# A convolutional attention kernel: column sums and divisors on quarters of TensorE's columns, inverses spread by DMA

## Chip, cores and metric

One core of a Trainium2 chip runs the whole kernel. The metric is the device time of one execution in microseconds (us). Three runs of the kernel before took 2658.37, 2661.5 and 2662.64 us; the median is 2661.5.

## What is computed

Two layers work on x of shape (8, 512, 64, 64) in float32: 8 images of 512 channels and 4096 positions. The first is softmax attention over max-pooled keys and values, the second is linear attention with a feature map `delu`.

```python
def layer0(x):
    f = conv1x1(x, Wf, bf).reshape(b, c // 8, h * w)
    g = maxpool2x2(conv1x1(x, Wg, bg)).reshape(b, c // 8, hwp)
    v = maxpool2x2(conv1x1(x, Wh, bh)).reshape(b, c // 2, hwp)
    beta = softmax(einsum('bcn,bcm->bnm', f, g), axis=-1)
    o = einsum('bcm,bnm->bcn', v, beta).reshape(b, c // 2, h, w)
    return gamma * conv1x1(o, Wv, bv) + x

def layer1(x):
    Q, K, V = wq x + bq, wk x + bk, wv x + bv
    Qf, Kf = delu(Q).transpose(0, 2, 1), delu(K)
    KV = einsum('bmn,bcn->bmc', Kf, V)
    norm = 1.0 / einsum('bnd,bd->bn', Qf, sum(Kf, axis=-1) + EPS)
    return x + gamma[0] * einsum('bnd,bdc,bn->bcn', Qf, KV, norm)
```

Two kinds of inverses matter here: those of the softmax's sums over the 1024 keys (one for each position), and `norm`, those of the second layer's divisors (one for each position as well).

## The kernel before, in words

An image's 4096 positions are cut into 8 chunks of 512, so there are 64 chunks, `s` = 0 to 63, and `j` = `s` mod 8 is the chunk's place in its image. `step(s)` (the loop over steps is at the end of `run`) lists pieces of work with a due time `t` by `at(t, fn, ...)`, sorts them by `t` and emits them in this order. The order on each engine's queue is thus written out by hand. The due times only order the work; they start nothing.

One step mixes four stages for different chunks:

- Stage A, for a chunk 9 ahead: f and g (`a_fg`, L259) and the values (`a_h`, products H, L303), with the pooled values turned by a DMA transpose (`turn_v`, L358, SP's queue, t = 18.7) and joined by ScalarE (L363).
- For chunk n = s + 1: the weights E = exp of the scores (`weigh`, matmuls `s`, L394), their sum over the keys (`sum_of_e` on VectorE adds the 8 tiles into one, `total` sums over the partitions), the inverses (`invert`), a check value for each chunk (`look`) and the multiplication of E with the inverses in four blocks (`normalize_block`, L460). E has keys on partitions and positions along the free axis, so the inverse of a position has to be on every partition. `total` does this by a matmul with a 128x128 tile of ones: every row of its result is the sum.
- For chunk s: the attention (`attend`, products M1 to M7 of a 2x2 scheme with 7 products, L484, their sums on VectorE), the projection and the residual (`project`, products N, L547). ScalarE evicts N1 three times (L557), GpSimd adds that to `xb` (L560), VectorE adds the others (L563, L568). N6, N5 and N3 accumulate into N1's bank and wait for the evictions.
- Layer 1 for chunk s: features (`features`, matmuls pk, L593, which read the finished `xb`), and for chunk s - 1 the sum of K times x (`gather`, matmuls pg, L687, on two halves of TensorE's columns). For the image before (`b_c`): `normalize` makes the divisors of a pair of chunks (matmul pd, L770), inverts them (L774) and multiplies `qq` with them (L777). It runs at j = 0 for the image's first pair and at j = 1, 3, 5 for the next pair. `finish` at odd j multiplies with KV (matmuls pa, L795), ScalarE copies to `y` (L798), and GpSimd's queue stores 1 MB twice with an accumulating DMA (L801, t = 12.6 and 14.3).

SP's queue issues the other DMAs in order: an output store (L574), loads of the next chunks (L212, L224), four transposes of x and one of k (L648, L630), one of v (L358). A wait of one of them holds all behind it.

Tiles come from pools: `bank` gives one of 8 PSUM banks, `scratch` one of 7 buffers of 128x512, `work1` one buffer for each tag. In the last image (s = 56 to 63) stage A is over and the steps are shorter; the features move into the next step.

After `run`, VectorE tests all of the check values against a limit (`good`, `least`, `bad`), and a second, general version of the whole program is branched over when they are in order, as they are here.

Of the kernel before, what the change touches and what calls it, by code (L numbers as in the profile page):

```python
# [36 lines left out]
F32 = mybir.dt.float32  # L37
U16 = mybir.dt.uint16
AF = mybir.ActivationFunctionType
ALU = mybir.AluOpType  # L40
AX = mybir.AxisListType

PARAM = 10.0
EPS = 1e-10
P = 128
CH = 512
SAFE = 1e27

# [2 lines left out]
def tile_two_attention_blocks(  # L51
# [72 lines left out]
    ident = const.tile([P, P], F32, name="ident")  # L124
# [38 lines left out]
    chk = const.tile([P, 2, TOTAL], F32, name="chk")  # L163

    def half(e):
        return slice(e * D, (e + 1) * D)

    def run(ctx, general):
# [6 lines left out]
        work1 = ctx.enter_context(tc.tile_pool(name="work1", bufs=1))  # L175
        work = ctx.enter_context(tc.tile_pool(name="work", bufs=2))
        temp = ctx.enter_context(tc.tile_pool(name="temp", bufs=7))
        turned = ctx.enter_context(tc.tile_pool(name="turned", bufs=1))
        small = ctx.enter_context(tc.tile_pool(name="small", bufs=4))
        psum = ctx.enter_context(tc.tile_pool(name="psum", bufs=8, space=bass.MemoryType.PSUM))  # L180

        def bank(name):
            return psum.tile([P, CH], F32, tag="m", name=name)

        def scratch(name):
            return temp.tile([P, CH], F32, tag="t", name=name)

# [38 lines left out]
        st = {}  # L226
        fgs, fs, vps = {}, {}, {}

        th, hs, es, sums, totals, rtots, te, os_, to, ns = ({} for _ in range(10))
        pxs, x_last, stored, late = [], {}, {}, {}  # L230
        kTs, xTs, pks, qq, halves, turned_halves = ({} for _ in range(6))

# [204 lines left out]
                nc.vector.tensor_tensor(r[:, 0, :], r[:, 0, :], r[:, 1, :], ALU.add)  # L437

        def total(s):
            pt = totals[s] = bank(f"tot_{s}")  # L440
            nc.tensor.matmul(pt, ones, sums[s][:, 0, :], start=True, stop=True)  # L441

        def invert(s):

            rtots[s] = bank(f"rtot_{s}")
            nc.vector.reciprocal(rtots[s], totals[s])  # L446

        def look(s):
            pt = totals[s]
            nc.scalar.activation(pt, pt, AF.Copy, accum_out=chk[:, 0, s : s + 1])  # L450
            nc.scalar.activation(pt, rtots[s], AF.Copy, accum_out=chk[:, 1, s : s + 1])

        def block(s, i, j):

# [309 lines left out]
        def normalize(pair, at, t, t_invert, t_out):  # L764

            m = {}

            def product():
                m["pd"] = bank(f"pd_{pair}")
                nc.tensor.matmul(m["pd"], kb, qq[pair], start=True, stop=True)  # L770

            def inversion():
                m["rn"] = scratch(f"rn_{pair}")
                nc.vector.reciprocal(m["rn"], m["pd"])  # L774

# [117 lines left out]
        def step(s):  # L893
# [5 lines left out]
            pair = (b_c * NCHUNK + j) // 2  # L899
            work = []  # L900

            def at(t, fn, *args):
                work.append((t, len(work), fn, args))
# [50 lines left out]
                    turn_G(b_c, at, 19.5)  # L954
                    make_KV(b_c, at, 21.4, 30.0)
            if c_here and here and j == 0:
                normalize(pair, at, 5.6, 6.9, 13.2)
            if c_here and here and j % 2 == 1 and j < NCHUNK - 1:
                normalize(pair + 1, at, 3.5, 4.9, 4.95)
            if c_here and here and j % 2 == 1:  # L960
                finish(pair, (0, 1), at, 9.2)
                finish(pair, (2, 3), at, 10.9)
# [20 lines left out]
            if after:  # L983
                n = s + 1
                if here:
                    at(5.7, weigh_two, n, 0)
                    at(7.5, weigh_two, n, 2)
                    for m, t in ((2, 9.3), (4, 10.6), (6, 11.8), (8, 13.1)):
                        at(t, sum_of_e, n, m)

                if not here:
                    t, t_invert = 21.2, 21.25
                elif s == 0:
                    t, t_invert = 21.2, 22.6
                else:
                    t, t_invert = 16.1 if j % 2 == 1 and c_here else 17.85, 18.0
                at(t, total, n)
                at(t_invert, invert, n)
                if not general:
                    at(max(21.5, t_invert + 0.1), look, n)  # L1000
                at(24.3, normalize_block, n, 0, 1)
                at(26.0, normalize_block, n, 0, 0)
                at(27.3, normalize_block, n, 1, 1)
                at(29.2, normalize_block, n, 1, 0)
                at(33.6, sums_of_e, n, 1)
                at(36.0, sums_of_e, n, 2)
# [65 lines left out]
        for s in range(-LEAD, TOTAL + 1):  # L1072
            step(s)
# [5 lines left out]
    with ExitStack() as stack, tc.manual_schedule(engines=ENGINES):  # L1079
        run(stack, general=False)  # L1080

    least = const.tile([1, 1], F32, name="least")
    good = const.tile([1, 2 * TOTAL], F32, name="good")
    nc.vector.tensor_scalar(good, chk[0:1].rearrange("p c s -> p (c s)"), SAFE, None, ALU.is_lt)
    nc.vector.tensor_reduce(least, good, AX.X, ALU.min)
    bad = const.tile([1, 1], mybir.dt.int32, name="bad")
    nc.vector.tensor_scalar(bad, least, 0.5, None, ALU.is_lt)
# [41 lines left out]
```

## Time and profile before

The profiled execution took 2656.62 us, its instructions span 2654.5 us; the difference lies before the first and after the last instruction.

| | before |
|---|---|
| median of three runs | 2661.5 us |
| profiled execution / its span | 2656.62 / 2654.5 us |
| TensorE matmul busy | 2606.4 us (98%) |
| VectorE busy | 2136.8 us (80%) |
| ScalarE busy | 1593.2 us (60%) |
| GpSimd busy | 763.5 us (29%) |
| mean granted TensorE clock | 0.994 |
| reciprocal of the sums (L446), 64 times | 3365 ns each |
| reciprocal of the divisors (L774), 28 times | 3351 ns each |
| `look`'s two passes (L450, L451) | 589 and 582 ns each |
| DMA, mean over the span | 139 GB/s |

How to read it: a float32 matmul appears as two passes, so 64 matmuls are 128 records. Passes overlap at their ends, so the pace of TensorE is read from one start to the next: a pass of 512 columns takes 0.43 us, one of 256 columns 0.216. In the lines of a timeline the columns are the start, the duration (both us), engine, line, operation, output<-inputs, shape and the number of merged instructions; in brackets stands the idle time before and what ended it. In lists of waits the numbers are us in total, times, and the longest. PE is TensorE, DVE VectorE, ACT ScalarE, POOL GpSimd and SP SyncE.

### The profile page before, as it was taken

The page shows a single profiled execution, that of the slowest core. Times are in us where ns is not written, and L with a number is a line of the kernel's source. Part 1 is how long each engine was busy: PE and PEld are TensorE (multiplying, and loading weights), DVE is VectorE, ACT ScalarE, POOL GpSimd, SP SyncE. Part 2 cuts the span into 40 slices and gives each one's busy share as a digit, 9 for nine tenths or more (in the row PEclk, how much of TensorE's full clock was granted, in tenths as well). Part 3 has the DMA queues.
Part 4 walks back from the last instruction along what each step waited for, and adds up shares of the span by engine and source line. Part 5 has one row for each costly group of instructions (what it writes and reads, how often), then busy time and mean ns, then how long its engine had stood idle before and what let it go on. Part 6 is the DMA issues. An engine that isn't in the chain of part 4 may idle for free.

```text
span 2654.5 us, 30415 instructions
## 1 busy us (share of the span) xinstructions
PE 2606.4 (98%) x10650; PEld 1798.1 (68%) x10650; DVE 2136.8 (80%) x2990; ACT 1593.2 (60%) x2670; POOL 763.5 (29%) x610
## 2 busy tenths in 40 slices
PE   8899999999999999999999999999999999999996
PEld 6577666667667667667667676666676676666663
DVE  5788879878888878887888888888788788798873
ACT  3365566566566566575675665666665656756661
POOL 4422323322322323223333223323223232221112
PEclk9999999999999999999999999999999999999998
DMA  5143455465555565655664654756555656455657
GB/s 172 49 134 89 115 135 149 104 164 134 133 157 118 142 167 118 164 133 116 152 162 121 155 125 123 180 116 151 141 118 158 155 119 159 117 138 138 154 144 256
DMA packets 465363, 369.91 MB, mean 139 GB/s; under 512 B 339888, under 2 KB 340400, under 8 KB 465200
## 3 DMA queue, kind: packets, MB, share of 16 engines
q1 hardware_dynamic: 444816, 307.16, 42.6%
q0 software_dynamic: 15232, 58.72, 12.0%
q10 hardware_dynamic: 5152, 1.97, 0.3%
q8 instruction: 87, 1.43, 0.2%
q14 instruction: 76, 0.62, 0.1%
HBM read 151.92 MB, written 134.22 MB: 108 GB/s over the span
## 4 chain that ended last, share of the span: by engine, by line
PE 87%; DVE 6%; DMA 1%; issue 1%; ACT 1%; POOL 0%; SPq 0%; DVEq 0%; POOLq 0%; ACTq 0%
PE M L484 27%; PE N L547 14%; PE H L303 11%; PE s L394 8%; PE pk L593 7%; PE fg L259 7%; PE pg L687 4%; PE pa L795 3%; PE tot L441 2%; PE pkv L752 1%; PE pd L770 1%; DMA xb<-in_x_dram 1%; DVE T L469 1%; DVE T L466 1%; DVE r L434 0%
## 5 line engine op out<-in xcount | busy, mean ns | idle before, releaser
L560 POOL TENSOR_TENSOR xb<-xb,n 128x512 f32<-128x512 f32 x192 | 246.7, 1285 | 553.3 <-ACT n L557 504.2
L484 PEld LDWEIGHTS M<-T,S 128*128 128x128 f32 x1536 | 286.5, 190 | 114.3 <-issue 29.2
L557 ACT ACTIVATE n<-N,gb_v 128x256 f32<-128x256 f32 x384 | 161.2, 471 | 334.1 <-PE N L547 333.2
L484 PE MATMUL M<-T,S 128*128 128x256 f32 x1536 | 358.7, 383 | 0.0
L655 ACT COPY xT<-u 128x1024 uint16<-128x1024 uint16 x252 | 328.2, 1353 | 1.4
L460 DVE TENSOR_TENSOR E<-E,rtot 128x1024 f32<-128x1024 f32 x256 | 305.2, 1214 | 3.8 <-issue 1.6
L642 ACT COPY w<-xb 128x1024 uint16<-128x1024 uint16 x252 | 244.8, 1042 | 81.8 <-DVE xb L563 81.8
L398 ACT ACTIVATE E<-s 128x512 f32<-128x512 f32 x512 | 256.1, 615 | 48.3 <-PE s L394 40.6
L446 DVE RECIPROCAL rtot<-tot 128x512 f32<-128x512 f32 x64 | 215.3, 3365 | 49.4 <-PE tot L441 49.4
L547 PE MATMUL N<-to,w_v 128*128 128x256 f32 x1024 | 243.6, 381 | 3.2 <-ACT n L557 3.0
L563 DVE TENSOR_TENSOR xb<-xb,N 128x512 f32<-128x512 f32 x256 | 175.0, 684 | 84.2 <-POOL xb L560 81.9
L394 PE MATMUL s<-f,g 64*128 64x512 f32 x1024 | 238.1, 602 | 1.9 <-DVE o L493 1.9
L593 PE MATMUL pk<-xb,w_kqk 128*128 128x512 f32 x512 | 231.8, 595 | 8.0 <-DVE xb L568 8.0
L634 POOL COPY kT<-uk 128x512 uint16<-128x512 uint16 x56 | 53.1, 949 | 620.6 <-DMA uk<-wk 620.6
L484 PE MATMUL M<-E,vT 128*128 128x256 f32 x1024 | 231.5, 379 | 0.0
L450 ACT ACTIVATE tot<-tot 128x512 f32<-128x512 f32 x64 | 37.7, 589 | 320.0 <-DVE rtot L446 319.9
L547 PEld LDWEIGHTS N<-to,w_v 128*128 128x128 f32 x1024 | 194.3, 191 | 30.8 <-ACT n L557 4.4
L484 PEld LDWEIGHTS M<-E,vT 128*128 128x128 f32 x1024 | 194.6, 190 | 29.4 <-issue 1.9
L259 PE MATMUL fg<-xa,w_fg 128*128 128x512 f32 x472 | 213.9, 596 | 0.0
L547 PE MATMUL N<-o,w_v 128*128 128x256 f32 x768 | 187.7, 380 | 1.9 <-ACT n L557 1.9
L547 PEld LDWEIGHTS N<-o,w_v 128*128 128x128 f32 x768 | 145.1, 190 | 54.8 <-issue 24.2
L394 PEld LDWEIGHTS s<-f,g 64*128 64x128 f32 x1024 | 94.7, 186 | 116.5 <-issue 90.6
(149 smaller groups left out, 4647.8 us busy)
## 6 DMA issues: line engine op xcount, KB each, us to landing
xb<-in_x_dram SPq DMA_DIRECT2D x64, 1024.0 KB, 5.7
out_dram<-xb SPq DMA_DIRECT2D x64, 1024.0 KB, 5.3
xa<-in_x_dram SPq DMA_DIRECT2D x59, 1024.0 KB, 7.4
out_dram<-y POOLq DMA_DIRECT2D x56, 1024.0 KB, 11.4
w_v<-in_L_conv_wv_dram SPq DMA_DIRECT2D x8, 1024.0 KB, 8.1
x_early<-in_x_dram SPq DMA_DIRECT2D x4, 1024.0 KB, 5.7
u<-w SPq DMA_TRANSPOSE x252, 3.3
x<-out_dram SPq DMA_DIRECT2D x12, 256.0 KB, 10.7
```

The source lines that it names most:

```text
L259: nc.tensor.matmul(fg, w_fg[:, k, :], x_a[a][:, k, :], start=(k == 0), stop=(k == KT - 1))
L303: nc.tensor.matmul(m[i], w_h7[i][:, k, :], th[a][i][:, k, :], start=(k == 0), stop=(k == hk - 1))
L394: nc.tensor.matmul(sc[e], g[half(e), i, :], fs[s][half(e), :], start=True, stop=True)
L398: nc.scalar.activation(es[s][:, 2 * i + e, :], sc[e], AF.Exp)
L446: nc.vector.reciprocal(rtots[s], totals[s])
L460: nc.vector.tensor_tensor(b, b, r, ALU.mult)
L484: nc.tensor.matmul(m[i], v7[i][:, k, :], te[s][i][:, k, :], start=(k == 0), stop=(k == hm - 1))
L547: nc.tensor.matmul(a[:, k, :], w_v7[i][:, bass.ts(k, P)], b, start=not more and k == 0, stop=True, skip_group_check=more or k > 0,)
L560: nc.gpsimd.tensor_tensor(of_x(*ij), of_x(*ij), u, ALU.add)
L593: nc.tensor.matmul(pk, w_kqk[:, i, e * D : (e + 2) * D], x_b[s][:, i, :], start=(i == 0), stop=(i == KT - 1),)
L642: nc.scalar.copy(w, x_b[s][:, k, :].bitcast(U16).rearrange("p (n h) -> p h n", h=2))
L655: nc.scalar.copy(v[:, k], u)
```

## The change

Three parts:

1. The sums (`total`) and the divisors (`product` in `normalize`) are no longer made on 128 rows for 512 positions. TensorE's columns are used in quarters of 32: quarter `i` takes 32 columns of weights and the positions 128 i to 128 i + 127, and writes rows 32 i to 32 i + 31. The result is a 128x128 tile. For the divisors the 32 columns are the middle ones of `kb`, 16 of each of the two chunks.
2. The reciprocals run on the 128x128 tile and write SBUF (`rq`, one buffer for both uses). SP's queue then writes the few rows that differ to DRAM (4 rows of 512 bytes for the sums, 8 for the divisors) and reads them back to all partitions (one DMA for the sums, two for the divisors). ScalarE copies the sums' inverses into a PSUM bank (`keep_inverses`). `look` reads the smaller tiles.
3. The due times of the divisors' three pieces change, for j = 0 from 5.6, 6.9 and 13.2, for odd j from 3.5, 4.9 and 4.95, both to 12.65, 13.7 and 30.9. The test at the end covers all 128 rows, with one transpose on TensorE more.

```diff
         def total(s):
-            pt = totals[s] = bank(f"tot_{s}")
-            nc.tensor.matmul(pt, ones, sums[s][:, 0, :], start=True, stop=True)
+
+            pt = totals[s] = bank(f"tot_{s}")[:, 0:P]
+            for i in range(NT):
+                nc.tensor.matmul(
+                    pt[bass.ts(i, QP), :], ones[:, 0:QP], sums[s][:, 0, bass.ts(i, P)],
+                    start=True, stop=True,
+                )
 
         def invert(s):
-
-            rtots[s] = bank(f"rtot_{s}")
-            nc.vector.reciprocal(rtots[s], totals[s])
+            rq[s] = work1.tile([P, P], F32, tag="rq", name=f"rq_{s}")
+            nc.vector.reciprocal(rq[s], totals[s])
+
+        def spread_inverses(s):
+
+            d = rows.tile([NT, P], F32, tag="rd", name=f"rd_{s}")
+            nc.sync.dma_start(out=d, in_=rq[s][0:P:QP, :])
+            u = rtots[s] = scratch(f"rb_{s}")
+            nc.sync.dma_start(out=u, in_=d.rearrange("(o i) n -> o (i n)", o=1).to_broadcast([P, CH]))
+
+        def keep_inverses(s):
+            u, rtots[s] = rtots[s], bank(f"rtot_{s}")
+            nc.scalar.copy(rtots[s], u)
 
         def look(s):
             pt = totals[s]
             nc.scalar.activation(pt, pt, AF.Copy, accum_out=chk[:, 0, s : s + 1])
-            nc.scalar.activation(pt, rtots[s], AF.Copy, accum_out=chk[:, 1, s : s + 1])
+            nc.scalar.activation(pt, rq[s], AF.Copy, accum_out=chk[:, 1, s : s + 1])
...
             def product():
-                m["pd"] = bank(f"pd_{pair}")
-                nc.tensor.matmul(m["pd"], kb, qq[pair], start=True, stop=True)
+
+                pd = m["pd"] = bank(f"pd_{pair}")[:, 0:P]
+                for i in range(NT):
+                    nc.tensor.matmul(
+                        pd[bass.ts(i, QP), :], kb[:, D - QP // 2 : D + QP // 2],
+                        qq[pair][:, bass.ts(i, P)], start=True, stop=True,
+                    )
 
             def inversion():
-                m["rn"] = scratch(f"rn_{pair}")
-                nc.vector.reciprocal(m["rn"], m["pd"])
+                rd = work1.tile([P, P], F32, tag="rq", name=f"rq_pd_{pair}")
+                nc.vector.reciprocal(rd, m["pd"])
+                d = rows.tile([2 * NT, P], F32, tag="rn", name=f"rn_{pair}_row")
+                nc.sync.dma_start(out=d, in_=rd[0 : P : QP // 2, :])
+                rn = m["rn"] = scratch(f"rn_{pair}")
+                for e in range(2):
+                    row = d.rearrange("(i e) n -> e i n", e=2)[e : e + 1]
+                    nc.sync.dma_start(
+                        out=rn[half(e)].rearrange("p (i n) -> p i n", n=P),
+                        in_=row.to_broadcast([D, NT, P]),
+                    )
...
             if c_here and here and j == 0:
-                normalize(pair, at, 5.6, 6.9, 13.2)
+                normalize(pair, at, 12.65, 13.7, 30.9)
             if c_here and here and j % 2 == 1 and j < NCHUNK - 1:
-                normalize(pair + 1, at, 3.5, 4.9, 4.95)
+                normalize(pair + 1, at, 12.65, 13.7, 30.9)
...
                 at(t, total, n)
                 at(t_invert, invert, n)
+                at(t_invert + 0.01, spread_inverses, n)
+                at(max(23.0, t_invert + 0.02), keep_inverses, n)
...
-    least = const.tile([1, 1], F32, name="least")
-    good = const.tile([1, 2 * TOTAL], F32, name="good")
-    nc.vector.tensor_scalar(good, chk[0:1].rearrange("p c s -> p (c s)"), SAFE, None, ALU.is_lt)
+    least = const.tile([P, 1], F32, name="least")
+    good = const.tile([P, 2 * TOTAL], F32, name="good")
+    nc.vector.tensor_scalar(good, chk.rearrange("p c s -> p (c s)"), SAFE, None, ALU.is_lt)
     nc.vector.tensor_reduce(least, good, AX.X, ALU.min)
+    with tc.tile_pool(name="row", bufs=1, space=bass.MemoryType.PSUM) as last:
+        row = last.tile([1, P], F32, name="row")
+        nc.tensor.transpose(row, least, ident)
+        nc.vector.tensor_reduce(least[0:1], row, AX.X, ALU.min)
```

The number `QP` is 32, `NT` is 4, `D` is 64, `P` is 128 and `CH` is 512. `rows` is a pool of DRAM tiles with two buffers for each tag.

More of the change, by code (lines that the diff above doesn't have):

```diff
@@ L45 @@
 P = 128
+QP = 32
 CH = 512
@@ L179, in run @@
         small = ctx.enter_context(tc.tile_pool(name="small", bufs=4))
+        rows = ctx.enter_context(tc.tile_pool(name="rows", bufs=2, space=bass.MemoryType.DRAM))
         psum = ctx.enter_context(tc.tile_pool(name="psum", bufs=8, space=bass.MemoryType.PSUM))
@@ L227, in run @@
         fgs, fs, vps = {}, {}, {}
-        th, hs, es, sums, totals, rtots, te, os_, to, ns = ({} for _ in range(10))
+        th, hs, es, sums, totals, rq, rtots, te, os_, to = ({} for _ in range(10))
         pxs, x_last, stored, late = [], {}, {}, {}
@@ L1080, in tile_two_attention_blocks @@
         run(stack, general=False)
-    least = const.tile([1, 1], F32, name="least")
-    good = const.tile([1, 2 * TOTAL], F32, name="good")
-    nc.vector.tensor_scalar(good, chk[0:1].rearrange("p c s -> p (c s)"), SAFE, None, ALU.is_lt)
+    least = const.tile([P, 1], F32, name="least")
+    good = const.tile([P, 2 * TOTAL], F32, name="good")
+    nc.vector.tensor_scalar(good, chk.rearrange("p c s -> p (c s)"), SAFE, None, ALU.is_lt)
     nc.vector.tensor_reduce(least, good, AX.X, ALU.min)
+    with tc.tile_pool(name="row", bufs=1, space=bass.MemoryType.PSUM) as last:
+        row = last.tile([1, P], F32, name="row")
+        nc.tensor.transpose(row, least, ident)
+        nc.vector.tensor_reduce(least[0:1], row, AX.X, ALU.min)
     bad = const.tile([1, 1], mybir.dt.int32, name="bad")
-    nc.vector.tensor_scalar(bad, least, 0.5, None, ALU.is_lt)
+    nc.vector.tensor_scalar(bad, least[0:1], 0.5, None, ALU.is_lt)
     again = nc.values_load(bad, min_val=0, max_val=1, skip_runtime_bounds_check_because="0 or 1")
```

## The prediction

> **What bounds the kernel now.** I read the page first: busy shares, then the chain that ended last.
>
> ```profile
> PE 2606.4 (98%) x10650; PEld 1798.1 (68%) x10650; DVE 2136.8 (80%) x2990; ACT 1593.2 (60%) x2670; POOL 763.5 (29%) x610
> ...
> PE 87%; DVE 6%; DMA 1%; issue 1%; ACT 1%; POOL 0%; SPq 0%; DVEq 0%; POOLq 0%; ACTq 0%
> ```
>
> TensorE (PE) is 98% busy and carries 87% of the chain. Next I asked for its waits, and for its instructions in one step in which divisors are made and outputs finished (j = 1, about 1424 to 1466 us).
>
> ```profile
> PE pk L593 <- DVE xb L568: 8.0, 2, 6.6
> ...
> 1433.46 3.60 PE L795 MATMUL pa<-qq,kv 64*128 64x512 f32 x16
> 1436.99 1.94 PE L687 MATMUL pg<-xT,kT 128*64 128x512 f32 x8
> 1438.86 1.99 PE L484 MATMUL M<-T,S 128*128 128x256 f32 x8
> 1440.69 1.02 PE L441 MATMUL tot<-r,ones 128*128 128x512 f32 x2
> 1441.55 3.62 PE L484 MATMUL M<-T,S 128*128 128x256 f32 x16
> ```
>
> The longest item in PE's list of waits is 8.0 us in the whole run, so PE is fed everywhere and time taken off it is time taken off the kernel, while nothing else comes late. What can come late is seen on VectorE (DVE) in the same step:
>
> ```profile
> 1441.82 3.37 DVE L446 RECIPROCAL rtot<-tot 128x512 f32<-128x512 f32 x1 [0.51 <-PE tot L441]
> ...
> 1448.84 1.21 DVE L460 TENSOR_TENSOR E<-E,rtot 128x1024 f32<-128x1024 f32 x1
> ...
> 1459.23 0.87 DVE L568 SCALAR_TENSOR_TENSOR xb<-N,gb_v,xb 128x256 f32<-128x256 f32 x2
> ```
>
> The line at L568 ends at 1460.10 and the features' matmuls, which read its xb, start at 1460.52: 0.4 us of slack. Last, the DMAs of that step:
>
> ```profile
> q1 hardware_dynamic: 5665, 4.15, 34.6%
> q0 software_dynamic: 544, 2.10, 27.2%
> ...
> out_dram<-y POOLq DMA_DIRECT2D x2, 1024.0 KB, 10.3
> ...
> uv<-wv SPq DMA_TRANSPOSE x1, 11.4
> ```
>
> In a step that finishes no outputs the same transpose lands sooner:
>
> ```profile
> uv<-wv SPq DMA_TRANSPOSE x1, 3.4
> ```
>
> The two accumulating stores of 1 MB (q0) make the difference. Packet by packet, q0 runs from 1439.1 to 1450.6 us with packets of 4 KB at 0.33 us each on all 16 engines. The transpose's 512 packets start only when the first store is complete and then go one for one with q0's (48 and 48 in a microsecond).
>
> **What the Trainium skill says.** (1) "TensorEngine Tiling (Array Packing)", Key Properties: tiles run in parallel, but a change of tiling mode drains the engine. The trace agrees with both. pg's 8 passes of 512 columns on two half-width tiles take 1.87 us (1436.99 to 1438.86), where eight in a row, as in tot (0.86 us for two), would take 3.44. The two changes of mode around pg cost 0.34: pa takes 3.53 where 8 x 0.43 = 3.44; pg 1.87 where 1.72; the M after it 1.83 where the M of 16 passes shows 3.45/2 = 1.73. (2) "TensorE: Matmul & The Clock Gate", Measured speedup vs the span model: three column tiles gave 2.38 times. No run here shows more than two. (3) "DMA: Bandwidth & Descriptors", Queues, rings and completion order: an engine takes the queue rows in turn and each ring in order. The one-for-one packets agree. (4) The clock gate page, Part 1: a window of idleness halves the clock. Here pauses of 2.95 us (to 92.3) and 3.38 us (to 133.2) were followed by a granted clock of 0.50.
>
> **The change, part by part.** Coordinates are those of the step shown.
>
> PE, sums. Before, 0.86 us (1440.69 to 1441.55). After, four tiles at once, two passes of 128 columns: half of the 0.216 us that a pass of 256 takes, twice, is 0.22; plus a way in and out, 0.34: 0.56. Gain 0.30 x 64 = 19. If the tiles ran one by one it were 0.86 + 0.34 = 1.20, a loss of 0.34.
> PE, divisors. Before, 0.85 us, alone among full-width work. Now they stand right behind pg, so only one more change of mode is paid: 0.22 + 0.15 = 0.37. Gain 0.48 x 28 (j = 0, 1, 3, 5 of seven images) = 13. Together 33 us off the bound engine.
>
> DVE, reciprocals. 3365 ns for 512 columns; a quarter of that, 0.85 to 0.9, for 128 (pure scaling at the low end). That frees 2.5 us in 64 + 28 places, 230 us in all, but DVE isn't the bound, and what it waits for next is the rows.
>
> ACT. Each look's two passes shrink from 0.59 towards a quarter; the new copy of rtot into a bank costs 0.59. ACT is at 60%: near nothing, except for its place in the order. Queued behind the waiting copy are the evictions of N1, and PE's N6, which accumulates into N1's bank, waits for the first of these.
>
> DMA on a free queue. Step by step: a store's first packet starts 1.0 us after its issue and it lands some 0.5 after the last packet (the 1 MB store at 1305.0: 1306.05, 1310.4). Row out: 1.6 to 2.3. Broadcast back: 128 packets of 2 KB, 8 on an engine at 0.085: 2.2 to 3. In the even steps the reciprocal ends 1.1 us after the sums, the copy takes 0.6, so the first normalization can start about 1.3 us earlier than now. Nothing is late; cost 0. The divisors' DMAs at j = 0 meet the weights' load, which ends about 1396.9 us while that step's normalizations start at 1404.5: also 0.
>
> DMA in the odd steps, where q0 is busy. SP's order is: divisors out, two broadcasts (rn), sums out, broadcast (rb), then the v transpose. Each waits on SP for the one it reads, and all behind it wait too.
> - The divisors' reciprocal ends near 1440.6. Their row lands between 1442.9 (if it only alternates with q0) and 1446 (if it is held as the transpose is).
> - rq is one buffer for both, so the sums' reciprocal waits on DVE until the divisors' row has left (1442.9 to 1446, then 0.9). Behind it stand the sums of M5, M7 and M4, which end at 1448.84 today and at 1450.7 at the latest, before N4 needs them (1451.0): 0.
> - rn: 2 x 64 partitions x 4 runs of 512 bytes = 512 packets, 32 on an engine. One for one with q0, only 9 to 18 of them get through before q0 ends (about 1450.9). The rest need under 1 us: 1451.5. Both bounds meet here, since q0's 32 packets on each engine take their 11 us either way.
> - The sums' row follows in the ring: landed 1452.0. rb is issued at 1452.1, first packet 1453.1, landed 1454.4. Copy to 1455.1.
> - Normalization starts at 1455.15, not 1448.84. From there to the end of L568 lie 11.26 us today, of which 2.05 idle (0.31, 0.56, 1.18), plus the multiplication with rn (0.92, L777), which is moved from an idle place to 30.9: 10.1. L568 ends at 1465.3, not 1460.1; less 0.4 slack, 4.8 us of stall. Inside it lies the pause at N6: due at 1452.75, possible at 1456.0 behind copy and eviction. At 3.2 us it is as long as the pauses that halved the clock; I add 0.2. So 5.0 x 21 (j = 1, 3, 5) = 105.
> At j = 7 there are no divisors. The row goes out near 1.4 us after the sums and rb has 8 packets on an engine at 0.41: rows land 0 to 1 us too late, 0.4 x 7 = 3.
>
> The rest. rn holds a scratch buffer of seven until 30.9, but the seventh buffer after it is asked for only at 35; the bank of rtot is taken later than now: 0. The wider test at the end, a transpose and two short reductions: under 1 us; taken as 1.
>
> Sum: -33 + 105 + 3 + 1 = +76 on the profiled execution's 2656.6 us (span 2654.5), so 2732. That execution lies 5 us under the median of 2661.5, so in terms of the median 2737.
>
> **Rivals.** Likeliest (0.70): the rows are late in the odd steps, 2737. With 3.3 to 7 us of stall in 21 steps (69 to 147) it spans 2699 to 2780.
> Faster (0.15): the rows are in time, because small copies pass the accumulating stores, or rn's packets don't hold up the sums' row. Then 33 - 1 are gained: 2629. It decides at 1449.7: if rb has landed by then in such a step, the normalization starts by 1450.3, and 1448.84 + 0.4 + 2.05 - 0.92 is the latest that costs nothing. For it: a free queue needs only some 5 us. Against it: uv's 11.4 us.
> The tiles don't do what they say (0.10): four columns in turn, each with its mode changes. PE loses 0.34 x 64 + 0.16 x 28 = 26 instead of gaining 33: 2737 + 59 = 2796. Against it: pg's halves do overlap.
> Rows late in every step (0.05): if each DMA took over 4 us, as small ones at the start do (b_h, 4.2), the even steps would lose 1 to 2 us as well: 2770 to 2830.
>
> **How the numbers follow.** Predicted is the likeliest, 2737. The range leaves out the faster case and the far tails, and reaches to the others: 2678 to 2825. About 0.2% (5 us) is what a measurement of this kernel can tell from no change. Faster 0.15, the one case; same 0.02, a balance of gain and a stall of 1.5 us; slower 0.83.
>
> **What would show it.** Right: tot takes about 0.2 us of matmul starts and its neighbours 0.3 more; RECIPROCAL near 0.9 us; rb's landing 2 to 3 us in even steps; in odd steps rn's landing near 8 us or more; ACT's copy waits for rb, PE's N6 for ACT's n, pk for L568, some 5 us a step, in odd steps alone. Wrong: odd steps no longer than now, rb landed within 9 us of the sums everywhere, PE waits as few as before. Then q0 doesn't hold the rows up, and the time is near 2629.

## The result, and the profile after

| | before | after |
|---|---|---|
| median | 2660.45 us (four runs, 2658.37 to 2662.64) | 2791.77 us (four runs, 2788.79 to 2793.62) |
| after / before | | 1.0492, 95% interval 1.0474 to 1.0511 |
| profiled execution / its span | 2656.62 / 2654.5 us | 2791.18 / 2789.0 us |
| mean granted TensorE clock | 0.994 | 0.974 |

The kernel is 4.9% slower. The forecast of 2737 us has the right sign and the right place, but the loss is 131 us where 76 were forecast. The 2791.77 us lie within the forecast's range (2678 to 2825) and above 2780, where its likeliest case ends. The range reached further for rivals that did not come true, so it is luck that the result falls into this part. The page of the kernel after, with its busy times and the chain that ended last by engine and by line:

```profile
PE 2633.6 (94%) x11203; PEld 1801.2 (65%) x11203; DVE 1923.9 (69%) x2991; ACT 1589.8 (57%) x2734; POOL 760.2 (27%) x610
...
PE 65%; DMA 15%; DVE 8%; issue 4%; ACT 3%; POOL 1%; SPq 0%; DVEq 0%; POOLq 0%; ACTq 0%
PE M L501 18%; PE H L305 11%; PE N L564 11%; PE s L396 7%; PE pk L610 7%; DMA rn_row<-rq_pd 5%; DMA rb<-rd 4%; DMA rd<-rq 4%; PE pg L704 4%; PE fg L261 3%; PE pa L826 3%; DVE r L436 1%; DVE E L477 1%; ACT n L574 1%; ACT E L400 1%
```

PE carries 65% of the chain where it carried 87%, and the new rows carry 13%: `rn_row` (the divisors to DRAM), `rd` (the sums to DRAM) and `rb` (the sums back). Who waits for them is in the list of waits of the kernel after (us in total, times, longest):

```profile
ACT rtot L463 <- DMA rb<-rd: 348.2, 64, 10.7
...
DVE E L477 <- ACT rtot L463: 191.1, 63, 7.1
...
DVE rq L452 <- DMA rn_row<-rq_pd: 124.9, 27, 6.2
...
PE N L564 <- ACT n L574: 108.2, 43, 6.5
...
PE pk L610 <- DVE xb L585: 8.2, 2, 6.8
```

Read from the bottom: the features (pk) wait as little as before (8.0 us in two times then, 8.2 now), so that isn't where TensorE stops. It stops at N, 43 times, for ScalarE's eviction `n`, which stands behind ScalarE's copy `rtot`, which waits for the row.

Where the time went shows best by steps, from the first M1 to the next (change against before, both from the profiled executions; "short" steps are those where stage A is over):

| steps | number | forecast, each | measured, each | forecast, sum | measured, sum |
|---|---|---|---|---|---|
| j = 1, 3, 5, images 1 to 6 | 18 | +4.22 | +5.08 | +76.0 | +91.4 |
| j = 1, 3, 5, last image (short) | 3 | +4.22 | +8.24 | +12.7 | +24.7 |
| j = 7, five of them | 5 | +0.1 | +2.44 | +0.5 | +12.2 |
| j = 7 of image 6 (short) | 1 | +0.1 | +8.52 | +0.1 | +8.5 |
| j = 2, 4, 6, images 1 to 6 | 18 | -0.30 | -0.28 | -5.4 | -5.0 |
| j = 0, images 1 to 6 | 6 | -0.78 | -0.40 | -4.7 | -2.4 |
| the rest (start, image 0, the last image's even steps, tail) | | | | -3.1 | +5.1 |
| sum | | | | +76 | +134.5 |

The forecast's column is its own terms: -0.30 and -0.48 for TensorE's two gains, +5.0 for a stall, +0.4 at j = 7. The rest holds a start that is 5.25 us longer before the first M1; in the runs below it changes from -1 to +7 us with no relation to the edits, and its cause isn't settled.

One step of the kind shown for before (step 25, j = 1, which starts at 1136.99 us). TensorE after:

```profile
1149.33 1.94 PE L704 MATMUL pg<-xT,kT 128*64 128x512 f32 x8
1151.20 0.43 PE L789 MATMUL pd<-qq,kb 128*32 128x128 f32 x8
1151.56 1.99 PE L501 MATMUL M<-T,S 128*128 128x256 f32 x8
1153.48 0.43 PE L445 MATMUL tot<-r,ones 128*32 128x128 f32 x8
1153.84 3.72 PE L501 MATMUL M<-T,S 128*128 128x256 f32 x16
...
1164.28 1.03 PE L564 MATMUL N<-to,w_v 128*128 128x256 f32 x4
1168.90 2.56 PE L564 MATMUL N<-to,w_v 128*128 128x256 f32 x8 [3.59 <-ACT n L574]
```

The tiles on four quarters do overlap: eight passes of tot take 0.36 us (1153.48 to 1153.84), where eight passes of 128 columns one after the other would take 0.86 us, by the pace of 0.216 us for 256. Then comes the pause of 3.59 us in N. Its cause runs back through VectorE, ScalarE and SP. VectorE after:

```profile
1151.92 0.95 DVE L796 RECIPROCAL rq_pd<-pd 128x128 f32<-128x128 f32 x1
...
1159.74 0.96 DVE L452 RECIPROCAL rq<-tot 128x128 f32<-128x128 f32 x1 [5.73 <-DMA rn_row<-rq_pd]
...
1168.11 1.22 DVE L477 TENSOR_TENSOR E<-E,rtot 128x1024 f32<-128x1024 f32 x1 [4.09 <-ACT rtot L463]
```

ScalarE after:

```profile
1167.49 0.59 ACT L463 COPY rtot<-rb 128x512 f32<-128x512 f32 x1 [5.95 <-DMA rb<-rd]
1168.01 0.83 ACT L574 ACTIVATE n<-N,gb_v 128x256 f32<-128x256 f32 x2
```

SP's queue after, in this step, in an even step (j = 6, from 1352.39) and in the j = 7 that follows (from 1390.13):

```profile
1152.90 0.62 SPq L798 DMA_DIRECT2D rn_row<-rq_pd  x1
1159.67 1.37 SPq L802 DMA_DIRECT2D rn<-rn_row  x2
1161.14 0.56 SPq L457 DMA_DIRECT2D rd<-rq  x1
1163.97 0.35 SPq L459 DMA_DIRECT2D rb<-rd  x1
...
1368.94 0.56 SPq L457 DMA_DIRECT2D rd<-rq  x1
1370.61 0.34 SPq L459 DMA_DIRECT2D rb<-rd  x1
...
1407.74 0.54 SPq L457 DMA_DIRECT2D rd<-rq  x1
1413.30 0.34 SPq L459 DMA_DIRECT2D rb<-rd  x1
```

The distance from `rd` to `rb` is the time that a row of 2 KB takes to DRAM, since rb's DMA waits for it. It is 1.67 us in the even step and 5.56 at j = 7, where the accumulating stores run. By packets, the first one of the row leaves 1.2 us after its issue in the even step and 4.44 us after it at j = 7. I call this longer wait from the issue to the first packet, here 3.2 us more than on quiet engines, **the hold**. In the j = 1 step the divisors' row takes it (first packet 4.8 us after the issue), and all that stands behind it on SP takes it too.

Last, the clock. Windows of the kernel after, of one width, from the pause on (PE's busy time and matmuls, granted clock, DMA share, GB/s):

```profile
1165.00:1168.41 3.41, 0.31 (x2) 1.00 0.50 112
1168.41:1171.83 3.42, 2.93 (x10) 0.76 0.00 0
1171.83:1175.24 3.41, 3.41 (x14) 0.74 0.00 0
1175.24:1178.65 3.41, 3.41 (x17) 1.00 0.00 0
```

After the pause, a stretch of 3.41 us (1170.2 to 1173.6) ran at half clock. (The granted clock is 0.76 and 0.74 in the two windows that it lies in.) Between the start of image 1 and the last step there are 22 such stretches, 12 of 3.41 us and 10 of 6.83, 109 us in all; before there is none. At half speed 109 us do the work of 55, so up to 55 us are lost to the clock, about a third of what the odd steps and j = 7 lose.

### The profile page after: what moved, and what is told of

It is laid out like the page before. It is cut to its first block, busy times and chain, and to the rows that moved or that the text cites. A ratio compares the mean times of both kernels' runs of the same rounds, so it can differ in the third digit from the quotient of the medians.

```text
span 2789.0 us, 32021 instructions
## 1 busy us (share of the span) xinstructions
PE 2633.6 (94%) x11203; PEld 1801.2 (65%) x11203; DVE 1923.9 (69%) x2991; ACT 1589.8 (57%) x2734; POOL 760.2 (27%) x610
## 4 chain that ended last, share of the span: by engine, by line
PE 65%; DMA 15%; DVE 8%; issue 4%; ACT 3%; POOL 1%; SPq 0%; DVEq 0%; POOLq 0%; ACTq 0%
PE M L501 18%; PE H L305 11%; PE N L564 11%; PE s L396 7%; PE pk L610 7%; DMA rn_row<-rq_pd 5%; DMA rb<-rd 4%; DMA rd<-rq 4%; PE pg L704 4%; PE fg L261 3%; PE pa L826 3%; DVE r L436 1%; DVE E L477 1%; ACT n L574 1%; ACT E L400 1%
## 5 line engine op out<-in xcount | busy, mean ns | idle before, releaser
L564 PE MATMUL N<-to,w_v 128*128 128x256 f32 x1024 | 287.7, 424 | 106.5 <-ACT n L574 106.3
L501 PE MATMUL M<-T,S 128*128 128x256 f32 x1536 | 366.9, 389 | 0.0
L564 PEld LDWEIGHTS N<-to,w_v 128*128 128x128 f32 x1024 | 214.0, 214 | 157.6 <-ACT n L574 124.1
L463 ACT COPY rtot<-rb 128x512 f32<-128x512 f32 x64 | 37.7, 589 | 348.2 <-DMA rb<-rd 348.2
L434 DVE TENSOR_TENSOR r<-E 128x1024 f32<-128x1024 f32 x64 | 78.4, 1225 | 192.4 <-ACT E L400 192.4
L305 PE MATMUL H<-xa,w_h 128*128 128x256 f32 x708 | 180.7, 393 | 0.0
```

What stands on the lines that cost most here:

```text
L305: nc.tensor.matmul(m[i], w_h7[i][:, k, :], th[a][i][:, k, :], start=(k == 0), stop=(k == hk - 1))
L501: nc.tensor.matmul(m[i], v7[i][:, k, :], te[s][i][:, k, :], start=(k == 0), stop=(k == hm - 1))
L564: nc.tensor.matmul(a[:, k, :], w_v7[i][:, bass.ts(k, P)], b, start=not more and k == 0, stop=True, skip_group_check=more or k > 0,)
```

## Experiments

The theory (H): the rows are late because the accumulating stores (q0) are on the DMA engines when they are issued. The rivals: (R1) the queue on SP and the shared `rq` make the sums late, whatever q0 does; (R2) the small DMAs are slow by themselves, or the quarters cost TensorE what they save; (R3) the stores' large packets of 4 KB are what hold the small ones up.

### No stores, or later stores

First the stores were taken out altogether; the second layer's outputs are then not added.

```diff
             def out():
-                nc.gpsimd.dma_start(
-                    out=outr[b, :, ks[0] : ks[0] + 2, bass.ts(jp, 2 * CH)],
-                    in_=m["y"].rearrange("p k e n -> p k (e n)"), accum_op=ALU.add,
-                )
+                pass
```

> The changed kernel without the two accumulating stores of the second layer's outputs (they are left out, so those outputs are not added). Theory H (the rows are held up by the accumulating stores): without them the steps j = 1, 3, 5 fall from 47.0 to about 41.1 us, j = 7 from 43.5 to about 39.7, and the run takes about 2630. Rival Q (the sums' row is late because SP issues it behind the divisors' three DMAs and their waits, stores or not): j = 1, 3, 5 stay at 44 or more and the run at 2720 or more. Rival S (rows through DRAM are too slow by themselves): also no better than 2760.

Measured: 2635.22 us in one run, beside a median of 2659.08 for before on that chip. Steps against before: j = 1, 3, 5 -0.70, even -0.31, short odd -0.04, j = 7 -0.30, short j = 7 +1.28 (its trace has a stretch at half clock there, as in the run with the stores late everywhere, below). The chain by engine and PE's waits at N in this kernel:

```profile
PE 86%; DVE 5%; issue 2%; DMA 1%; ACT 1%; POOL 1%; DVEq 0%; POOLq 0%; ACTq 0%; SPq 0%
```

```profile
PE N L564 <- ACT n L574: 10.0, 8, 4.8
```

With SP's order and the shared `rq` unchanged, DMA's share falls from 15% to 1%, and TensorE's gain of some 0.7 us appears in the odd steps. R1 and R2 are out as the cause by themselves. But 59 MB of transfers are gone from the whole run as well (the tail behind the last step's start is 6.2 us shorter), so next the stores were kept and moved:

```diff
-            at(t + 3.4, out)
+            at(20.6 + 0.05 * ks[0], out)
```

> The changed kernel, whole, with the accumulating stores issued some 10 us later in the step (due at 20.6 and 20.7 instead of 12.6 and 14.3), after the rows have landed. Theory H: all stalls of the odd steps go, 2625 to 2640 us, faster than the kernel before. The moved stores may meet the transposes of x at the end of the step, which would cost up to 2 us in an odd step, 2690 at most. Rivals Q and S: 2760 to 2790 as changed.

Measured: 2668.96 us, ratio 1.0040 (1.0028 to 1.0053): above the expected time. Where stage A runs, the theory held: j = 1, 3, 5 at 41.15 us against 46.97 in the kernel after. But the three short odd steps stayed at +8.38 us each and the short j = 7 at +6.78. A due time orders the work and starts nothing: in those steps GpSimd has no sums of x ahead of the stores, so they left as early as before. So the due times were made to depend on the stage:

```diff
-        def finish(pair, ks, at, t):
+        def finish(pair, ks, at, t, t_out):
...
-            at(t + 3.4, out)
+            at(t_out, out)
...
-                finish(pair, (0, 1), at, 9.2)
-                finish(pair, (2, 3), at, 10.9)
+                finish(pair, (0, 1), at, 9.2, 20.6 if a < TOTAL else 25.8)
+                finish(pair, (2, 3), at, 10.9, 20.7 if a < TOTAL else 25.9)
```

> As the kernel with the stores issued later, but in the last image's odd steps and in the j = 7 step before it, where GpSimd has no sums of x to do and the stores therefore still left early, they are due at 25.8, behind GpSimd's first addition to xb. Theory H: the stalls left over there (3 steps of 8.4 us, and two pauses, 6 us, in j = 7 of the sixth image) go too: 2669 - 30, about 2637, every odd step at or below the kernel before's. If those stalls had another cause (the short steps themselves): 2665.

Measured: 2640.97 us, ratio 0.9938 (0.9925 to 0.9952). The short odd steps are back at before's length (0.00). The short j = 7 stays at +1.73: the trace has a stretch of 3.41 us at half clock there, behind pauses of 0.93 and 1.80 us, where before has pauses of 0.93 and 1.34 us without such a stretch. In exchange the last image's even steps are 2.82 us longer (TensorE pauses there 3.1 us a step, at tot and N, against 0.66 before), and its j = 0 2.39. Its chain by engine:

```profile
PE 82%; DVE 6%; DMA 3%; issue 3%; ACT 2%; POOL 1%; DVEq 0%; ACTq 0%; POOLq 0%; SPq 0%
```

With nothing but two due times changed, the kernel after goes from 4.9% slower to 0.6% faster than before. That settles H: the stores' place in time is the cause.

### Which of the two halves, and in which order

The sums alone (divisors and their due times as before):

```diff
-                pd = m["pd"] = bank(f"pd_{pair}")[:, 0:P]
-                for i in range(NT):
...
+                m["pd"] = bank(f"pd_{pair}")
+                nc.tensor.matmul(m["pd"], kb, qq[pair], start=True, stop=True)
...
-                normalize(pair + 1, at, 12.65, 13.7, 30.9)
+                normalize(pair + 1, at, 3.5, 4.9, 4.95)
```

> Only the sums are changed; the divisors are made, inverted and used as in the kernel before. Theory H: the odd steps j = 1, 3, 5 stall as j = 7 does in the changed kernel, about 3.8 us, because the sums' two DMAs meet the stores without any divisors' DMA ahead: steps of about 45.4 us, 28 x 3.8 - 19 more than before: about 2745. Rival Q: without divisors' DMAs ahead the steps j = 1, 3, 5 are as short as before, 41.6, and the run is at about 2660.

Measured: 2716.34 us in one run. j = 1, 3, 5 are 1.93 us longer than before, a stall of 2.2 with the gain of 0.30 added back. The list of waits of this kernel has PE at N:

```profile
PE N L564 <- ACT n L574: 59.5, 57, 4.2
```

More pauses than after (57 against 43), but about 1.0 us each instead of 2.5. Only two stretches at half clock follow, behind pauses of 4.17 and 3.35 us in short steps; behind those of up to 1.6 us there is none. I expected a longer stall: one hold leaves pauses that mostly don't reach the clock.

The divisors alone (`total`, `invert`, `look` and the test at the end as before, no rows for the sums):

```diff
-            pt = totals[s] = bank(f"tot_{s}")[:, 0:P]
-            for i in range(NT):
...
+            pt = totals[s] = bank(f"tot_{s}")
+            nc.tensor.matmul(pt, ones, sums[s][:, 0, :], start=True, stop=True)
...
-                at(t_invert + 0.01, spread_inverses, n)
-                at(max(23.0, t_invert + 0.02), keep_inverses, n)
```

> Only the divisors are changed (quarters, small reciprocal, rows through DRAM, the moved due times); the sums and their inverses are made as before. Theory H: rn lands late in the odd steps too, but nothing needs it before 30.9, so only the gain on TensorE shows, 0.48 us in 28 steps: about 2647. If the moved multiplication of 0.92 us on VectorE or the late rn costs something, the steps j = 1, 3, 5 are longer than 41.4 and the run takes 2660 to 2700.

Measured: 2639.42 us, ratio 0.9925 (0.9908 to 0.9941). j = 1, 3, 5 are 0.50 us shorter (forecast 0.48) and j = 0 1.09, more than its matmuls: the divisors' matmul no longer waits for `kb`, as it did six times before, for 3.1 us in all. Its page:

```profile
PE 2591.9 (98%) x10818; PEld 1791.6 (68%) x10818; DVE 2062.5 (78%) x2990; ACT 1593.2 (60%) x2670; POOL 763.2 (29%) x610
```

PE loses 14.5 us of busy time against before (2606.4) and stays 98% busy. The divisors' rows have till 30.9 to land and so never stall anyone. The same kernel again, on another chip:

> The kernel with only the divisors changed once more, on the chip of the two others: about 0.9925 of the kernel before, 2638 to 2641.

Measured: 2639.96 us, ratio 0.9934 (0.9919 to 0.9949).

Next, both halves, but the divisors' DMAs behind the sums' on SP and with a buffer of their own:

```diff
-                rd = work1.tile([P, P], F32, tag="rq", name=f"rq_pd_{pair}")
+                rd = m["rd"] = work1.tile([P, P], F32, tag="rqd", name=f"rq_pd_{pair}")
                 nc.vector.reciprocal(rd, m["pd"])
+            def spread_divisors():
+                rd = m["rd"]
                 d = rows.tile([2 * NT, P], F32, tag="rn", name=f"rn_{pair}_row")
...
+            at(18.05, spread_divisors)
```

> The changed kernel with the order on SP's queue turned: the sums' row and its broadcast first, the divisors' row and broadcasts behind (with a buffer of their own for the divisors' reciprocal). The accumulating stores stay where they were. Theory H with the wait passed along SP's queue as a second part: the steps j = 1, 3, 5 then stall only as with the sums alone changed, 43.8 - 0.5 = about 43.3 us instead of 47.0, and j = 7 stays at 42.3 to 43.5: about 2715 for the run. If the order on SP doesn't matter and the stores alone decide: 46 to 47, 2780.

Measured: 2708.78 us in one run; j = 1, 3, 5 at 43.33 us. SP's queue of this kernel in step 25 (from 1110.60):

```profile
1128.57 0.56 SPq L457 DMA_DIRECT2D rd<-rq  x1
1133.73 0.35 SPq L459 DMA_DIRECT2D rb<-rd  x1
1134.13 0.59 SPq L800 DMA_DIRECT2D rn_row<-rq_pd  x1
1137.85 1.29 SPq L804 DMA_DIRECT2D rn<-rn_row  x2
```

The sums' row goes first and still takes 5.2 us to DRAM. So the 5.82 us by which an odd step is longer than with late stores (46.97 against 41.15) fall into two parts: 3.64 us (46.97 less 43.33) from standing behind the divisors, and 2.18 us from the sums' own hold, each with what the clock adds. The order on SP and the shared buffer were changed together, so their shares in the 3.64 aren't told apart. R1 is a part of the cause, but only while the stores run.

### What the hold is

Each store cut into two of 512 KB, with packets of 2 KB:

```diff
-                nc.gpsimd.dma_start(
-                    out=outr[b, :, ks[0] : ks[0] + 2, bass.ts(jp, 2 * CH)],
-                    in_=m["y"].rearrange("p k e n -> p k (e n)"), accum_op=ALU.add,
-                )
+                for e in range(2):
+                    nc.gpsimd.dma_start(
+                        out=outr[b, :, ks[0] : ks[0] + 2, bass.ts(2 * jp + e, CH)],
+                        in_=m["y"][:, :, e, :], accum_op=ALU.add,
+                    )
```

> The changed kernel with each accumulating store of 1 MB cut into two of 512 KB, one for each chunk of the pair, so that its packets are 2 KB instead of 4. If a row's packets wait behind a fixed number of store packets already taken in by a DMA engine (about ten of 0.33 us), the wait of the sums' row at j = 7, 4.4 us from issue to first packet, shrinks by 1 to 2 us and the odd steps by as much or more: below 2760. If it waits for a fixed time or amount of bytes, or for the end of a whole store: no change in the wait, 2780 to 2800; for the end of a store, the wait shrinks too, but ends right at the first completion.

Measured: 2781.97 us in one run; j = 1, 3, 5 at 46.73 us, j = 7 at +2.57. SP's queue of this kernel in the same j = 7 (step 31, from 1388.57):

```profile
1406.18 0.54 SPq L457 DMA_DIRECT2D rd<-rq  x1
1411.74 0.34 SPq L459 DMA_DIRECT2D rb<-rd  x1
```

Again 5.56 us, with the first packet 4.6 us after the issue. In the six steps of j = 7 it is 4.2 to 5.3 us, against 4.4 to 4.5 in the kernel after; for the divisors' row in the 18 odd steps it is 3.7 to 4.1, against 4.4 to 4.9. Packets half as large change little, so R3 is out as the cause, and the hold isn't a fixed number of packets. Nor does it wait for the end of a store, as the forecast had supposed for the transpose. In the kernel after, at j = 7, packets of 4 bytes close the first store at 20.0 to 20.5 us from the step's start and the second at 25.1 to 26.3, and the row's first packet goes between them, at 22.05; in step 59 the divisors' row has its first packet at 18.3 us, while the first store is closed no sooner than 20.0. What is still held when the second store ends goes then: at j = 7 rb is issued at 23.17 and has its first packet at 25.10, and in the 18 odd steps no packet of rn goes before the first one that closes the second store (24.9 to 25.2). Whether the hold is a fixed time or a fixed number of bytes these runs can't tell.

### Only where no stores run

Divisors on quarters everywhere; the sums on quarters only in steps without stores:

```diff
+        def busy(s):
+            return s > NCHUNK and s % 2 == 0
...
+            if busy(s):
+                pt = totals[s] = bank(f"tot_{s}")
+                nc.tensor.matmul(pt, ones, sums[s][:, 0, :], start=True, stop=True)
+                return
...
+            if busy(s):
+                rq[s] = rtots[s] = bank(f"rtot_{s}")
+                nc.vector.reciprocal(rtots[s], totals[s])
+                return
...
-                at(t_invert + 0.01, spread_inverses, n)
-                at(max(23.0, t_invert + 0.02), keep_inverses, n)
+                if not busy(n):
+                    at(t_invert + 0.01, spread_inverses, n)
+                    at(max(23.0, t_invert + 0.02), keep_inverses, n)
```

> The divisors changed everywhere, the sums only in steps without accumulating stores; in the odd steps with stores the sums and their inverses are made as in the kernel before. Theory H: no row meets a store on the way to something that waits, so both gains show where they are made: 2639 - 0.3 x 36 = about 2628. Rival: the rows cost something in quiet steps as well, then 2640 or more.

Measured: 2644.84 us, ratio 0.9955 (0.9942 to 0.9969), 17 us more than expected. j = 1, 3, 5 -0.50 and even -0.31 are as expected; j = 0 is -0.47 where the divisors alone gave -1.09, the short j = 7 is +1.69 (again with a stretch of 3.41 us at half clock behind its pauses of 0.93 and 1.33 us), and start and tail are 4.9 us longer. So I put the sums' DMAs ahead of the divisors' here, with the edit of the run that did so above:

> The kernel with the sums changed in quiet steps only, and the sums' row and broadcast ahead of the divisors' DMAs on SP (separate buffers for the two reciprocals). At j = 0, where the sums' row waited behind the divisors' DMAs, the step falls from 43.1 to about 42.0 us, seven times; all else stays: about 2645 - 8 = 2637. If order and buffer don't matter at j = 0, 2645.

Measured: 2638.57 us, ratio 0.9930 (0.9916 to 0.9943), as expected. j = 0 is now -1.59: there the divisors' rows in front, with the shared buffer, had cost the step 1.1 us, with no store near. The short j = 7 is at 0.00, with no stretch at half clock.

### All of it, with the stores late

Late stores where stage A runs, the sums first on SP in every step, and the old sums in the last image's steps with stores:

```diff
         def busy(s):
-            return s > NCHUNK and s % 2 == 0
+            return s > TOTAL - NCHUNK - 1 and s % 2 == 0
...
-                finish(pair, (0, 1), at, 9.2)
-                finish(pair, (2, 3), at, 10.9)
+                finish(pair, (0, 1), at, 9.2, 20.6 if a < TOTAL else 12.6)
+                finish(pair, (2, 3), at, 10.9, 20.7 if a < TOTAL else 14.3)
```

> The whole change with three edits: the stores issued later (20.6 and 20.7) wherever stage A still runs, the sums' DMAs ahead of the divisors' on SP, and in the last image's odd steps and the j = 7 before it the sums made the old way. Theory H: j = 1, 3, 5 at 41.15, j = 0 at about 42.0, even steps at 37.3, no step above the kernel before's: 2660 - 13 - 10 - 5.5 - 1, about 2630, faster than every version so far. If the late stores push into the transposes at the end of a step, the steps behind are longer and the run stays at 2640.

Measured: 2694.61 us, ratio 1.0144 (1.0128 to 1.0159), far from what I expected. Odd steps are 0.78 us shorter, but the even steps, which nothing had disturbed so far, are 3.20 us longer: 57.5 us in 18 steps. SP's queue of this kernel in step 25 (from 1110.01), then a line of its list of waits:

```profile
1127.97 0.56 SPq L468 DMA_DIRECT2D rd<-rq  x1
1129.65 0.35 SPq L470 DMA_DIRECT2D rb<-rd  x1
1130.04 0.59 SPq L811 DMA_DIRECT2D rn_row<-rq_pd  x1
1132.51 1.30 SPq L815 DMA_DIRECT2D rn<-rn_row  x2
1133.85 3.18 SPq L360 DMA_TRANSPOSE uv<-wv  x1
```

```profile
ACT vT L365 <- DMA uv<-wv: 100.3, 20, 6.7
```

The sums are quick (1.68 us to DRAM). But the divisors' rows behind them make the v transpose, which is last, go out at 23.8 us from the step's start instead of right behind `rb`, and there it meets the late stores (first packet at 24.8). Its own first packet goes 5.55 us after its issue. ScalarE's vT waits for it 20 times, in this step until 39.5 us from its start, and what stands behind vT on ScalarE moves into the next, even step, where TensorE then pauses (1.1 us a step). The hold had moved from the rows to the transpose. The mend: in odd steps the divisors' DMAs stay ahead of the sums', at j = 0 they stay behind.

```diff
-            at(18.05, spread_divisors)
+            at(max(t_spread, t_invert + 0.01), spread_divisors)
...
-                normalize(pair, at, 12.65, 13.7, 30.9)
+                normalize(pair, at, 12.65, 13.7, 30.9, 18.05)
...
-                normalize(pair + 1, at, 12.65, 13.7, 30.9)
+                normalize(pair + 1, at, 12.65, 13.7, 30.9, 13.71)
```

> The whole change, with the stores issued later as long as stage A runs, the sums' DMAs first on SP at j = 0 alone (in the other steps the divisors' DMAs stay first, so that the v transpose leaves before the stores), and the old sums in the last image's steps with stores. Theory H with what the run before showed of the v transpose: j = 1, 3, 5 at 41.15, even steps at 37.3, j = 0 at 42.0: about 2630, faster than the kernel before by 1%. If the even steps behind late stores are long again (40.8), it is the stores and not the v transpose behind the divisors' DMAs, and the run takes 2690.

Measured: 2630.90 us (2625.82 to 2633.70), ratio 0.9888 (0.9871 to 0.9905): the fastest of all, 1.1% under before. Steps against before: j = 1, 3, 5 -0.76, even -0.31, j = 0 -1.52, j = 7 -0.30, short j = 7 0.00, short odd -0.40. Its page, with the busy times and the chain:

```profile
PE 2579.8 (98%) x11179; PEld 1776.7 (68%) x11179; DVE 1945.4 (74%) x2991; ACT 1588.9 (60%) x2730; POOL 759.1 (29%) x610
...
PE 89%; DVE 3%; issue 2%; DMA 1%; ACT 1%; POOL 0%; SPq 0%; DVEq 0%; POOLq 0%; ACTq 0%
```

It has 26.6 us less of PE than before and PE is 98% busy again: the gain that the forecast worked out is there, once the rows keep clear of the stores.

## Why the prediction was right, and where it was short

1. **TensorE's gains: right.** Sums: forecast 0.30 us, measured 0.28 to 0.31 in even steps. Divisors: forecast 0.48, measured 0.50 (the divisors alone, odd steps). "TensorEngine Tiling (Array Packing)" was a sound ground for the overlap; here it is seen on four column tiles in float32, which start 7 ns apart.
2. **VectorE: right.** 0.94 to 0.96 us for a reciprocal (forecast 0.85 to 0.9), and 213 us of its busy time gone (2136.8 to 1923.9), without effect, as it isn't the bound.
3. **Even steps at no cost: right.** In step 30 the normalization starts 22.3 us from the step's start, and TensorE has no pause in that step.
4. **Lateness in odd steps: right.** The normalization was forecast at 31.36 us from the step's start (1455.15 less 1423.79), and step 25 has it at 31.12 (1168.11 less 1136.99). The divisors' row had been held, somewhat beyond the later of the forecast's two bounds (its broadcasts are issued at 22.7 us, the bound was 1446 less 1423.79, so 22.2), and the sums' reciprocal waited for the shared `rq` 5.73 us. The way there differed: the forecast let 9 to 18 of rn's 32 packets on an engine share with q0, one for one; in fact none went before the second store began to end at 25.05 us. The last went at 26.8, where the forecast had 27.7 (1451.5 less 1423.79), so its sum didn't suffer.
5. **The stall of 5.0 us: short.** The forecast took the end of L568 as the binding wait and the pause at N6 as lying inside it. It is the other way round: pk doesn't wait, N does (the pause of 3.59 us against a forecast of 3.2). And what follows the pause was mis-sized: 0.2 us for the clock. "TensorE: Matmul & The Clock Gate", Part 1, gives a window of 3413 ns; the trace agrees, each stretch at half clock being one or two of 3.41 us. 4.17 us of it fall on an odd step, which at half speed lose 2.1 us. Pause and clock make 3.7 + 2.1 = 5.8 us on the mean of the 18 steps, beside the 5.86 by which they exceed the forecast without a stall (46.97 less 41.11). PE's busy time agrees: it is 2633.6 us here and 2579.8 in the mended kernel, 54 us less, about half of the 109 at half clock. The split between the two is read from the trace; no run changed the clock alone. Two small slips stand in the forecast's working: the 0.92 us for L777 is a mean that counts 1.76 us at j = 0, while in the step shown it takes 0.69; and a stall of 69 to 147 us gives 2701 to 2779, where 2699 to 2780 is written.
6. **j = 7 at 0.4 us: wrong.** This is the term that was furthest off. The forecast let the row go out 1.4 us after the sums, as on a free queue, and then share the engines one for one with q0. But a DMA that is issued under the stores first waits out the hold: 5.56 us instead of 1.67 to rb's issue, then 4.8 instead of 3.5 us until ScalarE may copy. The normalization started 28.55 us from the step's start, not 24.2 as before. The forecast had the hold before its eyes, in the line of the transpose in the kernel before:

```profile
1440.24 1.65 SPq L358 DMA_TRANSPOSE uv<-wv  x1
```

Its first packet goes at 1445.08, 4.84 us after the issue, and the first store is closed from 1444.83 on. The forecast took the second for the reason of the first (the packets "start only when the first store is complete"), didn't price the 4.84 us, and used the end of the store as one end of a range for the divisors' row alone. Where it let small transfers share with q0 one for one from the start, rb and rn shared nothing, as shown above.
7. **The same sum for short steps: wrong.** Without stage A an odd step lost 8.24 us, and the short j = 7 8.52, where 5.0 and 0.4 were forecast. In the three odd ones the pauses are 6.5 us and the stretches at half clock 6.8 us a step, so 3.4 lost. Together that is 9.9, beside 9.0 to explain (8.24 and the gain of 0.78), so the sum of pause and clock fits less well there. That stage A's matmuls are what covers the difference elsewhere is argued, not shown.
8. **j = 0 at no cost: wrong by 0.4 us.** Without a store near, the divisors' rows in front of the sums' cost them; in the other order, and with a buffer of its own, the step gains 1.2 us more (-1.59 against -0.40).
9. **The rivals.** "Faster" gave 2629 us for rows that come in time, and the mended kernel, which keeps the old sums in four steps, comes near it (2630.9). Its condition, rb landed 25.9 us from the step's start (1449.7 less 1423.79), is missed in the kernel after by 4.6 us, since rb is there at 30.5. Tiles in turn and rows late in every step didn't occur.

## What to carry to other kernels

Here a round trip through DRAM to spread a few values was cheap only on quiet DMA engines, so look at what runs on them at that moment, in each kind of step, and price the wait from issue to first packet apart from the packets themselves. When an edit shifts a transfer, follow everything behind it on the same queue, for the next one may meet what the first one avoided. And price a pause of the bound engine together with its clock afterwards: in the odd steps here 3.7 us of pauses brought another 2.1 us at half clock, while with the sums alone pauses of up to 1.6 us brought none.

## What was unexpected of the hardware

- The hold: a DMA of SP's queue that is issued while the accumulating stores keep the engines busy has its first packet 4.4 to 4.9 us after its issue (the kernel after, j = 1, 3, 5 and 7 with stage A), against 1.2 us on quiet engines. With packets of 2 KB instead of 4 KB it is 3.7 to 5.3, and the end of the first of the two stores doesn't release it. In the kernel before, the transpose's packets, once begun, alternate with the stores'; in the kernel after rn (j = 1, 3, 5 with stage A) and rb (j = 7), issued some 2 to 3 us before the second store's end, get no packet through until then.
- A few long pauses cost more than many short ones. With one hold in the chain (sums alone) 57 pauses of 1.0 us on the mean gave two stretches at half clock; with two holds (the kernel after) 43 pauses of 2.5 us gave 22. The length alone doesn't decide it: in the kernel after a stretch followed a pause of 2.55 us (step 15), and none followed those of 3.45 and 3.37 us (steps 11 and 35).
